# Moving the softmax's power of e behind the layer-norm statistics, and reordering the first tiles' copies, in a correlation and feed-forward kernel

## The chip, the cores and the metric

The kernel runs on one core of a Trainium2 chip. A core has five engines with an instruction queue each: TensorE (PE: matmuls and transposes, with PEld for its weight loads), VectorE (DVE), ScalarE (ACT), GpSimd (POOL) and SyncE (SP, which here only issues DMA transfers). Each engine runs its own queue strictly in order and waits for others by semaphores. The metric is the device time of one execution in microseconds (us).

## The reference

The input x is 2 x 2048 rows of 1024 floats, treated as 4096 rows. Each row is layer-normalised; then two things are made of it and multiplied.

```python
xn = layernorm(x)                              # over the 1024 columns
# s: autocorrelation of a row by FFT, its 6 largest lags, softmax over them,
#    and the sum of the row rolled by those lags with these weights
corr = irfft(rfft(xn) * conj(rfft(xn)))
weights, delay = top_k(corr, 6)
p = softmax(weights)
s = sum_k p[k] * roll(xn, -delay[k])
# g: a gated feed-forward net with rank-2 additions (LoRA); every weight is a
#    quarter-size matrix tiled four times: w = tile(wq, (1, 4))
lin = lambda x, wq, A, B: x @ w.T + 0.5 * (x @ A.T @ B.T)
g = silu(lin(silu(lin(xn, w1q, a1, b1)) * lin(xn, w3q, a3, b3), w2q, a2, b2))
out = x + s * g
```

All is float32.

## The kernel before, in words

**Tiles and macros.** The 4096 rows are worked in 8 macros of 512 rows, each of four tiles of 128 rows. For each macro there is a `Corr` object, which normalises, transposes, finds the lags and the softmax weights, and an `Ffn` object, which runs the feed-forward net. The two are pipelined: while the net of macro m runs, the `Corr` of macro m + 1 is prepared.

**Steps.** A macro is 15 steps (`STEPS`). Steps 0 to 9 each do two of the 20 large products of the first layer (`Ffn.up`, matmuls at L521), step 10 the rest of that layer (`up_rest`), steps 11 to 14 the second layer for one tile of rows each (`Ffn.down`, L589 and L600, then `out`). The schedule is manual: each engine executes its instructions in the order in which the Python code emits them. `plan` fills four lists for each step: `pre` is emitted before a step's matmuls, `mid` and then `half` between its two products, and `end` behind them. Between them stand the gathers: `begin` issues indirect DMAs from GpSimd's queue that fetch rolled rows (at most four in flight), and `sum` adds a fetched row to `s` (ScalarE for the first of six, L471, VectorE for the others, L474). `sums` says how many are added in a step, as a pair: between the products (with `half`), and at the end.

**A tile of the next macro.** `stats` computes mean and variance (VectorE, L171 to L175), then the reciprocal deviation with a power on GpSimd (L177) and the shift (L179, GpSimd). `norm` then normalises on ScalarE (L186), scales the row sum on GpSimd (`rest`, L187), folds halves of the row on VectorE (L191; L142 and L143 in `fold_a`, which give `yc`; L142 uses `rest`) and on GpSimd (L193; L131 and L132 in `fold_b`). `save` writes the row twice to DRAM for the gathers. `turn` transposes the folded tile on TensorE (L215), and ScalarE copies it out of PSUM. `power` multiplies with Fourier tables (L365, L366) and squares (L375 to L381), `lags` goes back to the correlation (L393 to L412), `search` takes the top values and their places (L419 to L423).

**Softmax.** `weights` subtracts the row's largest value (VectorE, L431) and raises e to the result on GpSimd (L433, 24 values per row). `weights_rest` adds up and divides on VectorE (L439 to L443). Before the change, `weights` of macro m + 1 is emitted at the very end of macro m's step 14, and `weights_rest` at the end of step 0 of macro m + 1. In macro 0 they stand in `half` of step 6 and `mid` of step 7.

**The first macro.** It has no earlier macro to hide under. `norm_first`, `back_first` and `turn_first` do its four tiles in the main body (L717 to L744), `fold_lora` sums LoRA inputs on GpSimd, `lora_sum_first` and `lora_first` compute the LoRA part. The weights of the first layer have to be lessened by their first column block once (`lessen`: L136 on VectorE, L137 on GpSimd, two of six parts before the steps begin). `yU` is a second copy of `yT` whose first row differs. Within macro 0 the lags of its own four tiles and the statistics of macro 1's four tiles share steps 0 to 8; `stats` and `norms` in `plan` give the places of the latter.

**At the end of the first layer** `up_rest` makes the last part (L559 to L566), `lora_mid` adds the LoRA part to it (L573, VectorE) and copies it (L576, ScalarE), and L600 multiplies it.

**PSUM.** Two banks (`bank`) serve transposes, powers and lags in turn; five others (`full`) serve the products of the net, which ScalarE seeds (L499) two products ahead.

Of the kernel before, what the change touches and what calls it, by code (L numbers as in the profile page):

```python
# [34 lines left out]
F32 = mybir.dt.float32  # L35
# [12 lines left out]
RT = 4  # L48
# [19 lines left out]
def block_kernel(ctx: ExitStack, tc: tile.TileContext, x, w13t, w0t, w5t, w2t, a13, b13, b5, a2t, tf, ti, pick, out):  # L68
# [23 lines left out]
    def full(name):  # L92

        return psf.tile([P, 512], F32, tag="psf", name=name)
# [61 lines left out]
    class Corr:  # L156
# [96 lines left out]
            nc.scalar.copy(self.yT[0:1, 0, :], acc[0:1, :])  # L253
            nc.scalar.copy(self.yU[0:1, :], acc[32:33, :])

        def again(self):

            self.yU = p1.tile([P, NR], F32, tag="yU", name=f"yU_{self.m}")
            nc.scalar.copy(self.yU, self.yT[:, 0, :])

# [18 lines left out]
        def turn_first(self, r, signs):  # L281
            m = self.m
            if r == 0:
                self.yT = p2.tile([P, 2, NR], F32, tag="yT", name=f"yT_{m}")
                self.cT = p1.tile([P, 2, NR], F32, tag="cT", name=f"cT_{m}")
                self.bT = p1.tile([P, 4, NR], F32, tag="bT", name=f"bT_{m}")
                self.some = p1.tile([P, NR], F32, tag="us", name=f"us_{m}")
            cols = slice(r * P, (r + 1) * P)
            b, yc, back = self.parts.pop(r)

            t = full(f"t1_{m}_{r}")
            for k, (at, sign) in enumerate(((0, 1), (1, 1), (2, 0), (1, 0))):
                for h, (src, e) in enumerate(((b, ident), (back, signs[sign]))):
                    times = bass.AP(src.tensor, src.offset + at, [list(src.ap[0]), [2, P]])
                    nc.tensor.matmul(t[:, k * P : (k + 1) * P], lhsT=times, rhs=e, start=(h == 0), stop=(h == 1))
            nc.scalar.copy(self.bT[:, :, cols], t.rearrange("p (k n) -> p k n", k=4))
            t = full(f"t0_{m}_{r}")
            for k in range(4):
                nc.tensor.transpose(t[:, k * P : (k + 1) * P], yc[:, k, :], ident)
            t3 = t.rearrange("p (k n) -> p k n", k=4)  # L300
            nc.scalar.copy(self.yT[:, :, cols], t3[:, 0:2, :])
            nc.scalar.copy(self.cT[:, :, cols], t3[:, 2:4, :])

        def lora_sum_first(self, r, count):
            cols = slice(r * P, (r + count) * P)
# [12 lines left out]
        def lora_first(self, ffn):  # L318

            m = self.m  # L320
            self.yU = p1.tile([P, NR], F32, tag="yU", name=f"yU_{m}")
            nc.gpsimd.tensor_copy(self.yU, self.yT[:, 0, :])
            self.second = p1.tile([P, 2, NR], F32, tag="second", name=f"second_{m}")
            self.u = p1.tile([P, NR], F32, tag="u", name=f"u_{m}")
            self.pwy = p1.tile([P, 2, NR], F32, tag="pwy", name=f"pwy_{m}")
            ec = p1.tile([P, NR], F32, tag="ec", name=f"ec_{m}_0")
            e2 = p1.tile([P, NR], F32, tag="e2", name=f"e2_{m}_0")
            o2 = p1.tile([P, NR], F32, tag="o2", name=f"o2_{m}_0")

            def on_all(i):  # L330

                acc = full(f"second_{m}_{i}")
                col = pick_sb[:, 2 * i + 1 : 2 * i + 2]
                every = bass.AP(col.tensor, col.offset, [list(col.ap[0]), [0, P]])
                nc.tensor.matmul(acc, lhsT=every, rhs=self.some, start=True, stop=True)
                return acc

            e = full(f"fe_{m}_0")
            nc.tensor.matmul(e, lhsT=tf_sb[:, 0, :], rhs=self.yT[:, 0, :], start=True, stop=True)
            nc.scalar.copy(ec, e)  # L340
            nc.scalar.activation(e2, e, AF.Square)
            gate = on_all(0)
            nc.vector.tensor_copy(self.second[:, 0, :], gate)
            acc = full(f"u_{m}")
            nc.tensor.matmul(acc, lhsT=pick_sb, rhs=self.some, start=True, stop=True)
            nc.vector.tensor_copy(self.yT[0:1, 0, :], acc[0:1, :])
            nc.vector.tensor_copy(self.yU[0:1, :], acc[32:33, :])
            nc.vector.tensor_copy(self.u, acc)
            o = full(f"fo_{m}_0")
            nc.tensor.matmul(o, lhsT=tf_sb[:, 1, :], rhs=self.yT[:, 1, :], start=True, stop=True)  # L350
            nc.vector.tensor_tensor(self.pwy[:, 1, :], ec, o, ALU.mult)
            up = on_all(1)
            ffn.seed(0, (0,))
            nc.scalar.copy(self.second[:, 1, :], up)
            ffn.seed(0, (1,))
            nc.scalar.activation(o2, o, AF.Square)
            nc.gpsimd.tensor_tensor(self.pwy[:, 0, :], e2, o2, ALU.add)
            ffn.seed(1)
# [258 lines left out]
    def plan(m, st, nxt, after, gathers, ffn_next):  # L617

        pre, mid, half, end = ([[] for _ in range(STEPS)] for _ in range(4))
        first = m == 0  # L620
        sums = [(1, 0)] * 7 + [(1, 2)] * 3 + [(1, 1), (0, 0), (2, 1), (2, 1), (0, 0)]
        sums[10] = (0, 0)
        sums[0], sums[1] = (0, 0), (1, 1)
        sums[8], sums[9], sums[11], sums[14] = (2, 1), (2, 1), (1, 0), (1, 0)
        if first:
            sums = [(0, 0)] * 7 + [(1, 1), (2, 2)] + [(2, 1)] * 5 + [(3, 0)]
            mid[0].append(lambda: st.power(1))
            pre[1].append(lambda: st.power(2))
            mid[1].append(lambda: st.power(3))
            for r in range(RT):  # L630
                look(st, r, mid[2 + r], end[2 + r], gathers)
            half[2 + RT].append(st.weights)
            mid[3 + RT].append(st.weights_rest)
            for c in range(2, FULL + 1):
                pre[(0, 0, 1, 3)[c - 2]].append(lambda c=c: load_first(c))
                end[2 * c - 3].append(lambda c=c: lessen_part(c))
        else:
            end[0].append(st.weights_rest)
        if nxt is not None:
            if first:  # L640
                loads, norms, turns = (None, None, None, 3), (0, 1, 5, 6), (pre[6], mid[6], pre[7], pre[8])
                stats = (half[0], half[1], end[4], half[6])

                tags = (("yc", "bcs"), ("zf4", "zf5"), ("e2", "o2"), ("yc", "bcs"))
            else:
                loads, norms, turns = (None, None, 1, 3), (0, 2, 4, 6), (pre[2], pre[4], pre[6], pre[8])
                stats = (half[0], end[1], end[3], end[5])
                tags = (("yc", "bcs"),) * RT
            for r in range(RT):
                if loads[r] is not None:  # L650
                    pre[loads[r]].append(lambda r=r: nxt.load(r))
                stats[r].append(lambda r=r: nxt.stats(r))
                end[norms[r]].append(lambda r=r: (nxt.norm(r, tags[r]), nxt.save(r)))
                turns[r].append(lambda r=r: nxt.turn(r))
            mid[8].append(nxt.lora_sum)
            pre[9].append(lambda: nxt.power(0))
            mid[9].append(lambda: nxt.power(1))
            pre[10].extend([lambda: nxt.power(2), nxt.again])
            mid[10].append(lambda: nxt.power(3))
            pre[11].append(nxt.lora_spread)  # L660
            for r in range(RT):
                look(nxt, r, mid[MID + 1 + r], end[MID + 1 + r], gathers)
            end[STEPS - 1].append(nxt.weights)
            mid[STEPS - 1].insert(0, lambda: (ffn_next.seed(0), ffn_next.seed(1, (0,))))
            end[STEPS - 1].insert(0, lambda: ffn_next.seed(1, (1,)))
        if after is not None:
            pre[MID + 2].append(lambda: after.load(0))
            pre[MID + 4].append(lambda: after.load(1))
        return pre, mid, half, end, sums
# [24 lines left out]
    with tc.manual_schedule():  # L694
# [22 lines left out]
        constants()  # L717
        nc.gpsimd.memset(wide[:, 512:513], 0.0)
        nc.gpsimd.tensor_scalar(negative, ident, -1.0, None, ALU.mult)
        fold_lora(nat)  # L720
        bs = (b[:, :], wide[:, :])
        ycs = [p1.tile([P, 4, P], F32, tag=tag, name=f"yc_{tag}") for tag in ("yc", "zf0")]
        backs = [p1.tile([P, 257], F32, tag=tag, name=f"back_{tag}") for tag in ("bcs", "zf2")]
# [1 line left out]
        st.stats(0)  # L725
        st.stats(1)
        norm(0)
        st.back_first(0, backs[0][:, :])
        st.stats(2)
        norm(1)  # L730
        for r in range(RT):
            st.turn_first(r, (ident, negative))
            if r + 1 < RT:
                st.back_first(r + 1, backs[(r + 1) % 2][:, :])
            if r + 3 < RT:
                st.stats(r + 3)
            if r + 2 < RT:
                norm(r + 2)
            if r == 2:
                st.lora_sum_first(0, 3)  # L740
        st.lora_sum_first(3, 1)
        nc.vector.tensor_copy(basef, base)
        lessen_part(0)
        lessen_part(1)  # L744
        then.load(0)
# [156 lines left out]
```

## Time and profile before

| what | value |
|---|---|
| time, median of 3 runs | 1178.87 us (1176.96 to 1180.08) |
| the profiled execution: time, and span in its trace | 1178.45 us, 1176.7 us |
| granted TensorE clock, mean | 0.998 |
| TensorE busy | 1150.0 us (98%) |
| GpSimd busy | 783.2 us (67%) |
| VectorE busy | 738.7 us (63%) |
| ScalarE busy | 556.5 us (47%) |
| L433, the power of e, 8 times | 4202 ns each |
| L177, the power of the statistics, 32 times | 539 to 1559 ns, median 578 |
| first L521 matmul | starts at 34.22 us |
| a macro in steady state | 142.6 us from one L433 to the next (338.58 to 481.18) |

The times in the rows of the trace are counted in us from the start of the span. In a timeline row the first number is the start, the second the length, then engine, line, operation, output and input, shape; in brackets the idle time of that engine just before, and what ended it. In a row of waits the numbers are the total in us, how often, and the longest. The busy share is an average over 1177 us: which wait costs time has to be read at its place.

### The profile page before, as it was taken

What the parts mean: (1) busy time and instruction counts of PE and PEld (TensorE: products, weight loads), DVE (VectorE), ACT (ScalarE), POOL (GpSimd) and SP (SyncE); (2) the same over time, 40 slices, a digit from 0 to 9 for tenths busy, and PEclk for the clock granted to TensorE, in tenths of its full rate; (3) what the DMA queues carried; (4) which work ended last, traced back from release to release, by engine and by line L of the source; (5) the groups of instructions that cost most, each with busy time, mean ns of one, the idle gap of its engine ahead of it and who ended that gap; (6) DMA issues with size and microseconds to landing.
All of it is one profiled execution on the core that took longest, in us unless ns stands there. A gap on an engine that the chain in (4) does not pass through costs nothing.

```text
span 1176.7 us, 11238 instructions
## 1 busy us (share of the span) xinstructions
PE 1150.0 (98%) x3604; PEld 510.4 (43%) x3604; DVE 738.7 (63%) x985; ACT 556.5 (47%) x981; POOL 783.2 (67%) x643
## 2 busy tenths in 40 slices
PE   5999999999999999999999999999999999999997
PEld 4454344444444444444444444444444443444433
DVE  6587677664676557665576564675548664663455
ACT  4656425664256632565326652366433663344511
POOL 4668867777477755777558784597746877464653
PEclk9999999999999999999999999999999999999999
DMA  9942477533555435454365443654445534452334
GB/s 365 371 135 90 143 242 257 194 131 124 198 178 179 161 126 188 172 177 162 108 224 185 145 165 118 236 179 143 154 146 201 179 127 160 134 188 90 116 117 160
DMA packets 64915, 201.98 MB, mean 172 GB/s; under 512 B 7484, under 2 KB 7868, under 8 KB 64088
## 3 DMA queue, kind: packets, MB, share of 16 engines
q0 software_dynamic: 27648, 100.68, 26.0%
q1 hardware_dynamic: 37208, 100.59, 23.9%
q8 instruction: 28, 0.46, 0.2%
q14 instruction: 31, 0.25, 0.1%
HBM read 150.85 MB, written 50.39 MB: 171 GB/s over the span
## 4 chain that ended last, share of the span: by engine, by line
PE 85%; POOL 5%; DVE 4%; DMA 2%; ACT 2%; issue 1%; SPq 0%; POOLq 0%; DVEq 0%
PE gu L521 37%; PE y L589 24%; PE gu L547 5%; PE u L504 4%; PE y L600 3%; POOL e L433 3%; PE e L393 2%; PE fo L366 2%; PE fe L365 2%; PE t L215 2%; PE o L393 1%; DMA w<-in_w0t 1%; PE ua L231 1%; ACT x L186 1%; DVE where L421 1%
## 5 line engine op out<-in xcount | busy, mean ns | idle before, releaser
L521 PE MATMUL gu<-yT,w_sb 128*128 128x512 f32 x960 | 455.9, 596 | 0.0
L589 PE MATMUL y<-w_sb,zf 128*128 128x512 f32 x640 | 287.4, 596 | 0.0
L521 PEld LDWEIGHTS gu<-yT,w_sb 128*128 128x128 f32 x960 | 176.9, 190 | 227.2 <-issue 208.2
L457 POOL DMA_INDIRECT roll<-scr,lag x192 | 224.4, 1169 | 71.5 <-DVE s L474 28.8
L474 DVE SCALAR_TENSOR_TENSOR s<-roll,w,s 128x1024 f32<-128x1024 f32 x160 | 240.4, 1502 | 9.0 <-DMA roll<-scr,lag 4.1
L499 ACT ACTIVATE gu<-second,b_sb 128x512 f32<-128x512 f32 x320 | 207.6, 685 | 10.0 <-DVE z L528 9.4
L528 DVE TENSOR_TENSOR z<-z,gu 128x512 f32<-128x512 f32 x160 | 108.8, 683 | 159.3 <-PE gu L521 103.6
L613 POOL TENSOR_TENSOR g<-g,x 128x512 f32<-128x512 f32 x62 | 104.6, 1704 | 131.1 <-DVE g L612 108.7
L589 PEld LDWEIGHTS y<-w_sb,zf 128*128 128x128 f32 x640 | 117.3, 190 | 147.0 <-issue 146.3
L526 ACT ACTIVATE z<-gu 128x512 f32<-128x512 f32 x160 | 95.2, 595 | 167.5 <-PE gu L521 167.5
L521 PE MATMUL gu<-yU,w_sb 128*128 128x512 f32 x320 | 163.4, 592 | 0.0
L533 POOL TENSOR_TENSOR zf<-zf,z 128x512 f32<-128x512 f32 x80 | 133.6, 1670 | 19.6 <-DVE z L528 18.7
L531 POOL TENSOR_TENSOR zf<-z,z 128x512 f32<-128x512 f32 x40 | 50.7, 1266 | 76.6 <-DVE z L528 76.6
L521 PEld LDWEIGHTS gu<-yU,w_sb 128*128 128x128 f32 x320 | 60.8, 190 | 76.6 <-issue 72.5
L612 DVE TENSOR_TENSOR g<-s,g 128x512 f32<-128x512 f32 x64 | 41.5, 688 | 78.2 <-ACT g L611 78.2
L611 ACT ACTIVATE g<-y 128x512 f32<-128x512 f32 x64 | 34.7, 594 | 91.5 <-PE y L600 75.0
L547 PE MATMUL gu<-yT,w_sb 128*128 128x512 f32 x128 | 57.6, 593 | 0.0
L191 DVE TENSOR_TENSOR a<-x 128x512 f32<-128x512 f32 x28 | 32.8, 1172 | 29.6 <-ACT x L186 29.6
L504 PE MATMUL u<-z,a_sb 128*2 128x512 f32 (+1 forms) x384 | 49.9, 591 | 0.0
L412 ACT COPY corr<-corr 128x511 f32<-128x511 f32 x32 | 19.8, 618 | 63.2 <-DVE corr L411 63.2
L186 ACT ACTIVATE x<-x,shift,rstd 128x1024 f32<-128x1024 f32 x28 | 34.5, 1233 | 25.6 <-POOL shift L179 25.6
L375 ACT COPY ec<-fe 128x512 f32<-128x512 f32 x31 | 18.0, 581 | 60.0 <-PE fe L365 56.1
(168 smaller groups left out, 1262.8 us busy)
## 6 DMA issues: line engine op xcount, KB each, us to landing
scr<-x SPq DMA_DIRECT2D x64, 512.0 KB
x<-in_x SPq DMA_DIRECT2D x32, 512.0 KB
x<-in_x SPq DMA_DIRECT2D x64, 256.0 KB
out<-g SPq DMA_DIRECT2D x64, 256.0 KB
w_sb<-in_w13t SPq DMA_DIRECT2D x5, 1024.0 KB
second<-rows SPq DMA_DIRECT2D x14, 256.0 KB
w_sb<-in_w2t SPq DMA_DIRECT2D x1, 3072.0 KB
roll<-scr,lag POOLq DMA_INDIRECT x192, 5.9
```

Source lines behind the costliest of these rows:

```text
L457: nc.gpsimd.indirect_dma_start(out=g, out_offset=None, in_=st.scratch[r].rearrange("p (n o) -> (p n) o", o=1), in_offset=bass.IndirectOffs ...
L474: nc.vector.scalar_tensor_tensor(s, g, w, s, ALU.mult, ALU.add)
L499: nc.scalar.activation(acc, self.st.second[:, wi, :], AF.Copy, scale=b13_sb[:, c, q : q + 1])
L504: nc.tensor.matmul(self.u2[32 * j : 32 * j + 2, :], lhsT=a2_sb[:rows, 4 * c + j, :], rhs=z[:rows, :], start=(c == 0), stop=(c == FULL),)
L521: nc.tensor.matmul(acc, lhsT=w13_sb[:, c, 2 * j + wi, k, :], rhs=y, start=False, stop=(k == 1), skip_group_check=True,)
L526: nc.scalar.activation(z, accs[0], AF.Silu)
L528: nc.vector.tensor_tensor(z, z, accs[1], ALU.mult)
L531: nc.gpsimd.tensor_tensor(self.sum_of(c), zs[0], zs[1], ALU.add)
L533: nc.gpsimd.tensor_tensor(self.zf[c], self.zf[c], z, ALU.add)
L547: nc.tensor.matmul(acc, lhsT=w5_sb[:, k, j, :], rhs=self.st.yT[:, k, :], start=(k == 0), stop=False)
L589: nc.tensor.matmul(acc, lhsT=self.zf[c][:, rc], rhs=w2_sb[:, c, d * 512 : (d + 1) * 512], start=(c == 0), stop=False)
L613: (nc.vector if last else nc.gpsimd).tensor_tensor(g, g, xs[d], ALU.add)
```

## The change

The change edits the order in which instructions are emitted, and no arithmetic.

- In macros 1 to 7, `weights` moves from the end of the macro before to `half` of step 0, behind the statistics of the next macro's first tile, and `weights_rest` from the end of step 0 to `mid` of step 1. In macro 0, `weights` moves from `half` of step 6 to the end of step 5.
- In macro 0, `stats(2)` moves from the end of step 4 to the end of step 2, `norm(2)` from the end of step 5 to the end of step 4, `stats(3)` from `half` of step 6 to `half` of step 5; the sums of steps 8 to 11 change from (2, 2), (2, 1), (2, 1), (2, 1) to (2, 1), (1, 1), (2, 2), (2, 2).
- In the start, `turn_first` emits its TensorE work at once and returns its ScalarE copies as two functions, which the main body places: tile 2 is normalised between them, tile 3 ahead of tile 1's copies. `fold_lora` comes behind the first two tiles. The copy of `yU` goes into GpSimd's queue ahead of the lessening of the weights.

```diff
--- before.py
+++ after.py
@@ -253,10 +253,10 @@
             nc.scalar.copy(self.yT[0:1, 0, :], acc[0:1, :])
             nc.scalar.copy(self.yU[0:1, :], acc[32:33, :])
 
-        def again(self):
+        def again(self, copy=nc.scalar.copy):
 
             self.yU = p1.tile([P, NR], F32, tag="yU", name=f"yU_{self.m}")
-            nc.scalar.copy(self.yU, self.yT[:, 0, :])
+            copy(self.yU, self.yT[:, 0, :])
 
 
 
@@ -288,18 +288,24 @@
             cols = slice(r * P, (r + 1) * P)
             b, yc, back = self.parts.pop(r)
 
-            t = full(f"t1_{m}_{r}")
+            tb = full(f"t1_{m}_{r}")
             for k, (at, sign) in enumerate(((0, 1), (1, 1), (2, 0), (1, 0))):
                 for h, (src, e) in enumerate(((b, ident), (back, signs[sign]))):
                     times = bass.AP(src.tensor, src.offset + at, [list(src.ap[0]), [2, P]])
-                    nc.tensor.matmul(t[:, k * P : (k + 1) * P], lhsT=times, rhs=e, start=(h == 0), stop=(h == 1))
-            nc.scalar.copy(self.bT[:, :, cols], t.rearrange("p (k n) -> p k n", k=4))
+                    nc.tensor.matmul(tb[:, k * P : (k + 1) * P], lhsT=times, rhs=e, start=(h == 0), stop=(h == 1))
             t = full(f"t0_{m}_{r}")
             for k in range(4):
                 nc.tensor.transpose(t[:, k * P : (k + 1) * P], yc[:, k, :], ident)
-            t3 = t.rearrange("p (k n) -> p k n", k=4)
-            nc.scalar.copy(self.yT[:, :, cols], t3[:, 0:2, :])
-            nc.scalar.copy(self.cT[:, :, cols], t3[:, 2:4, :])
+
+            def copy_b():
+                nc.scalar.copy(self.bT[:, :, cols], tb.rearrange("p (k n) -> p k n", k=4))
+
+            def copy_y():
+                t3 = t.rearrange("p (k n) -> p k n", k=4)
+                nc.scalar.copy(self.yT[:, :, cols], t3[:, 0:2, :])
+                nc.scalar.copy(self.cT[:, :, cols], t3[:, 2:4, :])
+
+            return copy_b, copy_y
 
         def lora_sum_first(self, r, count):
             cols = slice(r * P, (r + count) * P)
@@ -318,8 +324,6 @@
         def lora_first(self, ffn):
 
             m = self.m
-            self.yU = p1.tile([P, NR], F32, tag="yU", name=f"yU_{m}")
-            nc.gpsimd.tensor_copy(self.yU, self.yT[:, 0, :])
             self.second = p1.tile([P, 2, NR], F32, tag="second", name=f"second_{m}")
             self.u = p1.tile([P, NR], F32, tag="u", name=f"u_{m}")
             self.pwy = p1.tile([P, 2, NR], F32, tag="pwy", name=f"pwy_{m}")
@@ -623,23 +627,21 @@
         sums[0], sums[1] = (0, 0), (1, 1)
         sums[8], sums[9], sums[11], sums[14] = (2, 1), (2, 1), (1, 0), (1, 0)
         if first:
-            sums = [(0, 0)] * 7 + [(1, 1), (2, 2)] + [(2, 1)] * 5 + [(3, 0)]
+            sums = [(0, 0)] * 7 + [(1, 1), (2, 1), (1, 1), (2, 2), (2, 2), (2, 1), (2, 1), (3, 0)]
             mid[0].append(lambda: st.power(1))
             pre[1].append(lambda: st.power(2))
             mid[1].append(lambda: st.power(3))
             for r in range(RT):
                 look(st, r, mid[2 + r], end[2 + r], gathers)
-            half[2 + RT].append(st.weights)
+            end[1 + RT].append(st.weights)
             mid[3 + RT].append(st.weights_rest)
             for c in range(2, FULL + 1):
                 pre[(0, 0, 1, 3)[c - 2]].append(lambda c=c: load_first(c))
                 end[2 * c - 3].append(lambda c=c: lessen_part(c))
-        else:
-            end[0].append(st.weights_rest)
         if nxt is not None:
             if first:
-                loads, norms, turns = (None, None, None, 3), (0, 1, 5, 6), (pre[6], mid[6], pre[7], pre[8])
-                stats = (half[0], half[1], end[4], half[6])
+                loads, norms, turns = (None, None, None, 3), (0, 1, 4, 6), (pre[6], mid[6], pre[7], pre[8])
+                stats = (half[0], half[1], end[2], half[5])
 
                 tags = (("yc", "bcs"), ("zf4", "zf5"), ("e2", "o2"), ("yc", "bcs"))
             else:
@@ -652,6 +654,10 @@
                 stats[r].append(lambda r=r: nxt.stats(r))
                 end[norms[r]].append(lambda r=r: (nxt.norm(r, tags[r]), nxt.save(r)))
                 turns[r].append(lambda r=r: nxt.turn(r))
+        if not first:
+            half[0].append(st.weights)
+            mid[1].append(st.weights_rest)
+        if nxt is not None:
             mid[8].append(nxt.lora_sum)
             pre[9].append(lambda: nxt.power(0))
             mid[9].append(lambda: nxt.power(1))
@@ -660,7 +666,6 @@
             pre[11].append(nxt.lora_spread)
             for r in range(RT):
                 look(nxt, r, mid[MID + 1 + r], end[MID + 1 + r], gathers)
-            end[STEPS - 1].append(nxt.weights)
             mid[STEPS - 1].insert(0, lambda: (ffn_next.seed(0), ffn_next.seed(1, (0,))))
             end[STEPS - 1].insert(0, lambda: ffn_next.seed(1, (1,)))
         if after is not None:
@@ -717,7 +722,6 @@
         constants()
         nc.gpsimd.memset(wide[:, 512:513], 0.0)
         nc.gpsimd.tensor_scalar(negative, ident, -1.0, None, ALU.mult)
-        fold_lora(nat)
         bs = (b[:, :], wide[:, :])
         ycs = [p1.tile([P, 4, P], F32, tag=tag, name=f"yc_{tag}") for tag in ("yc", "zf0")]
         backs = [p1.tile([P, 257], F32, tag=tag, name=f"back_{tag}") for tag in ("bcs", "zf2")]
@@ -725,21 +729,33 @@
         st.stats(0)
         st.stats(1)
         norm(0)
-        st.back_first(0, backs[0][:, :])
+        back = lambda r: st.back_first(r, backs[r % 2][:, :])
+        turn = lambda r: st.turn_first(r, (ident, negative))
+        back(0)
         st.stats(2)
         norm(1)
-        for r in range(RT):
-            st.turn_first(r, (ident, negative))
-            if r + 1 < RT:
-                st.back_first(r + 1, backs[(r + 1) % 2][:, :])
-            if r + 3 < RT:
-                st.stats(r + 3)
-            if r + 2 < RT:
-                norm(r + 2)
-            if r == 2:
-                st.lora_sum_first(0, 3)
+        back(1)
+        fold_lora(nat)
+        st.stats(3)
+        copy_b, copy_y = turn(0)
+        copy_b()
+        norm(2)
+        copy_y()
+        copies = turn(1)
+        back(2)
+        norm(3)
+        for copy in copies:
+            copy()
+        copies = turn(2)
+        back(3)
+        for copy in copies:
+            copy()
+        st.lora_sum_first(0, 3)
+        for copy in turn(3):
+            copy()
         st.lora_sum_first(3, 1)
         nc.vector.tensor_copy(basef, base)
+        st.again(nc.gpsimd.tensor_copy)
         lessen_part(0)
         lessen_part(1)
         then.load(0)
```

## The prediction

> **What bounds the kernel now.** I read the page's busy shares first, then TensorE's waits, then the timelines around each wait, engine by engine.
>
> ```profile
> PE 1150.0 (98%) x3604; PEld 510.4 (43%) x3604; DVE 738.7 (63%) x985; ACT 556.5 (47%) x981; POOL 783.2 (67%) x643
> PE t L295 <- POOL rest L268: 9.8, 1, 9.8
> PE t L215 <- DVE yc L143: 3.5, 7, 0.5
> PE t L215 <- DVE yc L142: 1.7, 1, 1.7
> PE fo L366 <- DVE pwy L378: 1.0, 1, 1.0
> ```
>
> TensorE is the bound: its work is unchanged, so only its waits can move the time. After the first matmul they are few: in the ready macros (m = 1 to 6) one of 0.5 us each, at `turn(0)`, and nothing else; in the first macro 2.2 at `turn(3)` (1.7 + 0.5), 1.0 in `power(1)`, 0.4 earlier; and holes in the start. So all that can be gained after the start is 6 x 0.5 + 3.6 = 6.6 us, while a step that becomes late in a ready macro costs six times.
>
> GpSimd (POOL), VectorE (DVE) and TensorE at the edge of macros 3 and 4 (start, length, engine, line):
>
> ```profile
> 481.18 4.20 POOL L433 TENSOR_TENSOR e<-euler,e 128x24 f32<-128x24 f32 x1 [0.35 <-DVE e L431]
> 485.37 0.54 POOL L177 TENSOR_TENSOR rstd<-var,mhalf 128x1 f32<-128x1 f32 x1
> 486.02 0.26 POOL L179 TENSOR_SCALAR shift<-mv,rstd 128x1 f32<-128x1 f32 x1
> 486.25 1.27 POOL L531 TENSOR_TENSOR zf<-z,z 128x512 f32<-128x512 f32 x1
> 487.74 0.73 POOL L187 TENSOR_SCALAR rest<-rest 128x1 f32<-128x1 f32 x1 [0.22 <-ACT x L186]
> ...
> 483.17 0.16 DVE L175 TENSOR_SCALAR var<-mv 128x1 f32<-128x1 f32 x1
> 487.68 0.69 DVE L191 TENSOR_TENSOR a<-x 128x512 f32<-128x512 f32 x1 [1.66 <-ACT x L186]
> 488.50 1.51 DVE L142 SCALAR_TENSOR_TENSOR yc<-a,rest 128x256 f32<-128x256 f32 x1
> 489.93 1.07 DVE L143 TENSOR_TENSOR yc<-a 128x256 f32<-128x256 f32 x1
> ...
> 491.06 0.44 PE L215 MATMUL t<-ident,yc 128*128 128x128 f32 x2 [0.49 <-DVE yc L143]
> ```
>
> The reader is to see a chain with no slack: `rest` (POOL) frees `yc` (DVE, 488.50), whose end frees the transposes. `rest` waited for ScalarE only 0.22 us; before it POOL was busy. All eight powers of e last 4.20 us.
>
> The start, and the tightest place of the first macro:
>
> ```profile
> 22.46 5.29 POOL L137 TENSOR_TENSOR w_sb<-w_sb,w 128x1024 f32<-128x1024 f32 x2
> 23.16 2.37 DVE L142 SCALAR_TENSOR_TENSOR yc_zf<-a,rest 128x256 f32<-128x256 f32 x1
> 25.45 2.58 DVE L143 TENSOR_TENSOR yc_zf<-a 128x256 f32<-128x256 f32 x1
> ...
> 151.57 1.27 DVE L474 SCALAR_TENSOR_TENSOR s<-roll,w,s 128x1024 f32<-128x1024 f32 x1
> 152.87 2.84 DVE L573 SCALAR_TENSOR_TENSOR zf<-u,zf 2x512 f32<-2x512 f32 x4
> 155.75 0.62 ACT L576 COPY zf<-zf 64x512 f32<-64x512 f32 x1 [7.93 <-DVE zf L573]
> ...
> 156.33 1.21 PE L600 MATMUL y<-w_sb,zf 64*128 64x512 f32 x4
> ```
>
> The lessening of the first weights (L137) meets the last tile's fold: L142 and L143 need 0.49 and 0.42 us elsewhere and take 4.95 here. And at 156.33 TensorE starts as its operand ends (156.37).
>
> **The change, part by part.** *(1) Power of e behind the statistics, macros 1 to 6.* Removed: 4.20 us ahead of `rstd`. Added: 4.20 us behind `shift`, with L531, `rest`, L193, L131, L132 queued behind it. Var is ready at 483.33; `rstd` (0.57, with hand-over 0.1) and `shift` (0.27) end at 484.2, so ScalarE normalises from 484.2 instead of 486.32 and its `x` is there at 485.6. But POOL is in the power from 484.2 to 488.4, and `rest` needs POOL. Does `a` (L191, two operands from SBUF) run meanwhile? L191 took 2.71 us at 58.82, when POOL's L137 (58.62, 2.36) had begun first, and ended 0.55 after it: it stood still for all of it. [...] No row shows the long power beside such an instruction. [...] power to 488.4, `a` to 489.0, L531 to 490.2, `rest` (0.24 where nothing hinders it, 93.57) to 490.5; L142 starts 2.0 us later than 488.50. Without it: L531 to 489.65, `rest` to 489.9; 1.4 later. I take 2.0. TensorE arrives at 490.16 in both cases and the wait has nothing beside it: 6 x 2.0 = **+12.0** (8.4 by the low end).
>
> [...]
>
> Weights_rest (three DVE instructions of 0.18) moves to mid[1], behind L142, L143 and z; ScalarE's first `s` waits for it until about 494.2 (it began at 489.26), with Silu and the seeds of the fifth product behind it, ready near 497.3; TensorE, itself 2.0 late, wants them at 498.5. Nothing added; if that cover fails, 0.5 to 1 us a macro.
>
> *(2) The start.* `fold_lora` (POOL 5.78 to 6.70) leaves the front: `rstd` starts at 5.9 instead of 6.66, everything 0.8 earlier. At its new place its four small POOL instructions meet L142/L143 of tile 1, and ScalarE's `a_sb` behind them (about 15.5) stands ahead of `copy_b(0)` and tile 2's `x`: tile 2 is normalised 0.7 later than before (15.34). Tile 3 gains: its `x` no longer waits behind copies (18.4 instead of 20.36), and the yU copy, now ahead of the lessening in POOL's queue, waits for the last yT, so the lessening can't meet the fold: L143 ends near 21.8 instead of 28.03. What is late next is ScalarE: back(3) and the copies of tiles 1 and 2 to about 22.2, the LoRA product (1.65) to 23.7, `turn(3)` (2.4) to 26.1, yT near 26.2 instead of 28.56. **-2.4**. The bounds: TensorE's holes from 9.8 to 34 add up to about 3.1, with the 0.8 at most -3.9; +0.5 if `a_sb` holds more. VectorE's lessening (2.8 us) moves to 22 to 25, free time. POOL's (2 x 2.4) runs from 27, the first done by 29.5, while the first product wants it near 32. SP issues the same transfers in the same order (each norm's two saves move along with it, past no other transfer); DMA is full until 55 us, but the next w0 tile, landing near 50 (19.4 MB moved by then), is wanted near 52.
>
> *(3) Norm(2) at end[4], stats(2) at end[2], stats(3) at half[5].* Norm(2) puts a 1.3 us pass on ScalarE and L191, L142, L143 (about 3.2 us [...]) on DVE ahead of z and corr of lag tile 3, while only stats(2) (1.7) leaves that spot. Corr ended at 87.37 and TensorE's `turn(0)`, which takes its bank of PSUM, came at 88.92: slack 1.55. I get corr 2.7 later: **+1.1** (0 to 2). Power(e) then starts some 3 us earlier against TensorE, and stats(3) is out of its way: `rest` of norm(3) ends near 104.9 instead of 106.57, TensorE arrives 1.1 later: of 2.2 at `turn(3)`, **-1.9**.
>
> *(4) Sums rearranged.* One `s` fewer at the end of step 8: `pwy` is no longer held by the 2.92 us `s` at 123.59: **-1.0**. One more `s` at the end of step 10 stands between L566 and L573 (the last of the rows above), where TensorE has 0.0 of slack: **+1.3**, by the 1.27 of the row; 0 if DVE has come free earlier[...].
>
> Sum: 12.0 - 2.4 + 1.1 - 1.9 - 1.0 + 1.3 = **+9.1**. The profiled execution took 1178.45 (span 1176.7), 0.4 under the median 1178.87: 1178.45 + 9.1 = 1187.5.
>
> **Rivals.** *Harmless power (not slower).* If the power is over before `rest` is wanted, the six waits vanish: 6 x -0.5 - 2.9 (the other five terms) = -5.9, 1172.5. It decides at a power of 4.2 - 2.0 = 2.2 us for no loss; for it speaks that `x` does come 2.1 earlier; against it that eight durations agree to 2 ns. Chance 0.09. *All of the first macro.* The start brings 3.9, (3) and (4) cost nothing and save 3.2[...]: 8.4 - 7.1 = +1.3, 1179.8, no change. Each is at its bound, so 0.08. *Knock-on.* The late `s` delays seeds or the next statistics: another 0.8 a macro, 9.1 + 4.8 = +13.9, 1192.4. For it speaks a slack of 1.2 us; chance 0.11. *As summed*, own range 1183 to 1190.5: 0.72.
>
> **How the numbers follow.** 1187.5 is the likeliest case. From 1181.5 (low end of the power's cost, larger gains at the start) to 1191.5 leaves out the first rival, most of the second and half of the third. A measurement here can tell about 0.3% (3.5 us): faster 0.09, within 0.08, slower 0.83.
>
> **What would show it.** Right: TensorE's waits at L215 for DVE yc grow to about 2.5 us each, six times; L433 starts behind L179; L142 of the last first-macro tile near 0.5 us; first L521 near 31.8 instead of 34.22; a wait of about 1.3 at L600 once. Wrong: L433 under 2.2 us, `rest` directly behind `shift`, or waits at L215 unchanged.

## The result, and the profile after

The changed kernel takes 1188.36 us (median of 6 runs, 1186.66 to 1188.77) against 1177.55 for the kernel before in the same comparison: ratio 1.0084, 95% interval 1.0071 to 1.0097. The time is inside the range, 0.9 us from the forecast. But two terms of the sum were off by about 5 and 3.5 us in opposite directions. The forecast also started from one execution of the kernel before, 1178.45, which was 0.9 us above the median; the difference itself is 10.8 us where 9.1 was forecast. So the closeness of the total is partly luck.

In kernels that contain the new start, lines from there on have moved, those from `weights` on by 4: the power of e is L437, the first layer's products are L525, L600 has become L604, L573 and L576 are L577 and L580, and the gathers and sums are L461, L475 and L478.

The page's busy shares and TensorE's waits of the kernel after:

```profile
PE 1153.0 (97%) x3604; PEld 511.0 (43%) x3604; DVE 733.1 (62%) x985; ACT 554.8 (47%) x981; POOL 785.0 (66%) x643
PE t L215 <- DVE yc L142: 8.4, 6, 1.8
PE t L215 <- DVE yc L143: 2.9, 6, 0.5
PE t L215 <- DVE corr L415: 1.3, 1, 1.3
PE y L604 <- DVE zf L577: 0.7, 1, 0.7
```

The reader is to see three things. A wait for L142 has come in each of the six ready macros. The waits at `turn(3)` and in `power(1)` are gone and two new ones of the first macro stand in their place. And TensorE is busy 3.0 us longer with the same 3604 instructions, which no list of waits explains.

The same place as in the prediction's timelines, which by the numbering from 0 is the edge of macros 2 and 3, in the timelines of GpSimd, VectorE and TensorE (start, length, engine, line):

```profile
484.96 0.26 POOL L179 TENSOR_SCALAR shift<-mv,rstd 128x1 f32<-128x1 f32 x1
485.19 4.18 POOL L437 TENSOR_TENSOR e<-euler,e 128x24 f32<-128x24 f32 x1
489.35 1.25 POOL L535 TENSOR_TENSOR zf<-z,z 128x512 f32<-128x512 f32 x1
490.59 0.23 POOL L187 TENSOR_SCALAR rest<-rest 128x1 f32<-128x1 f32 x1
...
486.63 0.69 DVE L191 TENSOR_TENSOR a<-x 128x512 f32<-128x512 f32 x1 [1.51 <-ACT x L186]
490.85 1.52 DVE L142 SCALAR_TENSOR_TENSOR yc<-a,rest 128x256 f32<-128x256 f32 x1 [3.53 <-POOL rest L187]
...
490.16 1.02 PE L525 MATMUL gu<-yT,w_sb 128*128 128x512 f32 x2
492.52 0.41 PE L215 MATMUL t<-ident,yc 128*128 128x128 f32 x2 [1.33 <-DVE yc L142]
493.41 0.44 PE L215 MATMUL t<-ident,yc 128*128 128x128 f32 x2 [0.49 <-DVE yc L143]
494.40 3.34 PE L525 MATMUL gu<-yT,w_sb 128*128 128x512 f32 x4
```

The power now stands between `shift` and `rest`. `x` is ready early, VectorE has `a` by 487.3, and then waits 3.53 us for `rest`. The last row is the surprise: the same four matmuls took 1.88 us before and take 3.34 now. The row of the kernel before:

```profile
492.04 1.88 PE L521 MATMUL gu<-yT,w_sb 128*128 128x512 f32 x4
```

The windows of 2 us over that place, in the kernel after (us, busy of PE, PEld, DVE, ACT, POOL, granted TensorE clock, DMA share, GB/s):

```profile
492.00:494.00 2.00, 0.99 (x6) 0.62 (x6) 2.00 (x4) 0.00 (x0) 1.92 (x3) 1.00 0.01 4
494.00:496.00 2.00, 1.95 (x6) 0.98 (x6) 1.27 (x3) 0.62 (x1) 1.83 (x3) 0.67 0.00 0
496.00:498.00 2.00, 2.00 (x4) 0.84 (x3) 0.96 (x2) 2.00 (x4) 0.66 (x2) 0.50 0.29 49
498.00:500.00 2.00, 2.00 (x8) 0.49 (x10) 2.00 (x3) 2.00 (x6) 2.00 (x1) 0.98 0.55 213
```

After the long wait TensorE's granted clock falls to half (0.67 and 0.50 in the second and third row) for 3.41 us. In this execution it happens in macros 1, 3 and 6; before the change no 2 us window ahead of the last matmuls shows it. From the first product to the matmul behind the two products' half (L508) it took 5.22 us (494.40 to 499.62) against 3.53 (492.04 to 495.57) before: 1.7 us for each drop.

The start: the last tile's fold no longer meets the lessening.

```profile
20.99 0.48 DVE L142 SCALAR_TENSOR_TENSOR yc_zf<-a,rest 128x256 f32<-128x256 f32 x1
21.39 0.42 DVE L143 TENSOR_TENSOR yc_zf<-a 128x256 f32<-128x256 f32 x1
...
31.70 1.88 PE L525 MATMUL gu<-yT,w_sb 128*128 128x512 f32 x4
```

And the end of macro 0's first layer, with two sums ahead of L577:

```profile
145.79 0.68 DVE L570 TENSOR_TENSOR zf<-zf,z 64x512 f32<-64x512 f32 x1 [2.21 <-POOL zf L569]
146.40 2.59 DVE L478 SCALAR_TENSOR_TENSOR s<-roll,w,s 128x1024 f32<-128x1024 f32 x2
149.03 2.84 DVE L577 SCALAR_TENSOR_TENSOR zf<-u,zf 2x512 f32<-2x512 f32 x4
...
151.93 1.77 PE L604 MATMUL y<-w_sb,zf 64*128 64x512 f32 x4 [0.71 <-DVE zf L577]
```

A cleaner measure than the listed waits is the distance, from start to start, of equal places. From the first matmul of step 11 (L589 or L593) to that of the next macro, in us:

| kernel | macro 0 to 1 | 1 to 2 | 2 to 3 | 3 to 4 | 4 to 5 | 5 to 6 |
|---|---|---|---|---|---|---|
| before | 142.68 | 142.60 | 142.59 | 142.61 | 142.58 | 142.61 |
| after | 147.50 | 143.94 | 145.67 | 143.97 | 143.95 | 145.68 |

Those with a clock drop are the first, third and last: 143.95 is a macro with the longer wait, 145.67 one with the wait and a drop.

### The profile page after: what moved, and what is told of

Read it like the earlier page. It is cut to its first block, busy times and chain, and to the rows that moved or that the text cites. A ratio compares the mean times of both kernels' runs of the same rounds, so it can differ in the third digit from the quotient of the medians.

```text
span 1186.5 us, 11239 instructions
## 1 busy us (share of the span) xinstructions
PE 1153.0 (97%) x3604; PEld 511.0 (43%) x3604; DVE 733.1 (62%) x985; ACT 554.8 (47%) x981; POOL 785.0 (66%) x643
## 4 chain that ended last, share of the span: by engine, by line
PE 85%; POOL 6%; DVE 5%; ACT 2%; issue 1%; DMA 0%; DVEq 0%; POOLq 0%
PE gu L525 39%; PE y L593 23%; PE gu L551 4%; PE u L508 4%; PE y L604 3%; PE e L397 2%; PE fe L369 2%; POOL e L437 2%; PE fo L370 2%; PE t L215 2%; PE o L397 1%; DVE stats L171 1%; PE ua L231 1%; DVE where L425 1%; DVE top L423 1%
## 5 line engine op out<-in xcount | busy, mean ns | idle before, releaser
L525 PE MATMUL gu<-yT,w_sb 128*128 128x512 f32 x960 | 460.4, 601 | 0.0
L593 PE MATMUL y<-w_sb,zf 128*128 128x512 f32 x640 | 287.4, 596 | 0.0
L525 PEld LDWEIGHTS gu<-yT,w_sb 128*128 128x128 f32 x960 | 178.1, 191 | 228.9 <-issue 208.5
L461 POOL DMA_INDIRECT roll<-scr,lag x192 | 218.6, 1138 | 71.5 <-DVE s L478 28.8
L478 DVE SCALAR_TENSOR_TENSOR s<-roll,w,s 128x1024 f32<-128x1024 f32 x160 | 236.4, 1477 | 5.4 <-DMA roll<-scr,lag 2.5
L593 PEld LDWEIGHTS y<-w_sb,zf 128*128 128x128 f32 x640 | 117.3, 190 | 147.1 <-issue 146.3
L525 PE MATMUL gu<-yU,w_sb 128*128 128x512 f32 x320 | 163.9, 594 | 0.0
L537 POOL TENSOR_TENSOR zf<-zf,z 128x512 f32<-128x512 f32 x80 | 138.8, 1736 | 26.8 <-DVE z L532 25.3
L525 PEld LDWEIGHTS gu<-yU,w_sb 128*128 128x128 f32 x320 | 61.5, 192 | 78.0 <-issue 73.1
L475 ACT ACTIVATE s<-roll,w 128x1024 f32<-128x1024 f32 x32 | 36.5, 1142 | 51.1 <-DVE w L447 49.7
L142 DVE SCALAR_TENSOR_TENSOR yc<-a,rest 128x256 f32<-128x256 f32 x28 | 40.9, 1461 | 30.7 <-POOL rest L187 28.7
L508 PE MATMUL u<-z,a_sb 128*2 128x512 f32 (+1 forms) x384 | 49.9, 591 | 0.0
L191 DVE TENSOR_TENSOR a<-x 128x512 f32<-128x512 f32 x28 | 31.1, 1110 | 24.6 <-ACT x L186 24.6
```

Source lines behind the costliest of these rows:

```text
L461: nc.gpsimd.indirect_dma_start(out=g, out_offset=None, in_=st.scratch[r].rearrange("p (n o) -> (p n) o", o=1), in_offset=bass.IndirectOffs ...
L478: nc.vector.scalar_tensor_tensor(s, g, w, s, ALU.mult, ALU.add)
L508: nc.tensor.matmul(self.u2[32 * j : 32 * j + 2, :], lhsT=a2_sb[:rows, 4 * c + j, :], rhs=z[:rows, :], start=(c == 0), stop=(c == FULL),)
L525: nc.tensor.matmul(acc, lhsT=w13_sb[:, c, 2 * j + wi, k, :], rhs=y, start=False, stop=(k == 1), skip_group_check=True,)
L537: nc.gpsimd.tensor_tensor(self.zf[c], self.zf[c], z, ALU.add)
L593: nc.tensor.matmul(acc, lhsT=self.zf[c][:, rc], rhs=w2_sb[:, c, d * 512 : (d + 1) * 512], start=(c == 0), stop=False)
```

## Experiments

Theory: the power of e in its new place costs, by holding GpSimd ahead of `rest` and by what TensorE's clock does after the longer wait; the start and the first macro gain. Rivals: the cost sits in the first macro; it is the order on other engines and not GpSimd's time; the clock drops are unrelated to the wait.

**The move of the power alone.**

```diff
-        else:
-            end[0].append(st.weights_rest)
...
+        if not first:
+            half[0].append(st.weights)
+            mid[1].append(st.weights_rest)
...
-            end[STEPS - 1].append(nxt.weights)
```

> The kernel before, with the move of the power of e in macros 1 to 7 alone (weights behind the statistics of step 0, weights_rest in the middle of step 1); start and first macro as before. Theory (the power costs, twice): TensorE's wait at L215 goes from 0.5 to 1.8 us in six macros, +8.0 to 8.4 us, and in two to four of the six the granted clock drops to about half for some 3.4 us after it, +1.7 us each: together +11.5 to +15, so 1189 to 1193. Rival (the added time sits in the changed start and first macro): within 3 us of the kernel before, about 1178.

Measured: 1187.5 us (1187.27 to 1190.25), ratio 1.0091, interval 1.0076 to 1.0107. The waits of the ready macros are those of the kernel after, 1.3 and 0.5 us, with those of the old first macro beside them. The macros are 143.94 to 144.06 apart, one, with a clock drop, 145.66. The profiled run has that one drop, fewer than the two to four expected, and the median is 1.5 us under the expected band. Its row of waits, with macro 0's old wait as the seventh:

```profile
PE t L215 <- DVE yc L142: 9.5, 7, 1.7
```

The cost of the change is in this edit; the rival is out.

**The start and first macro alone** (the kernel after with the power back).

```diff
+        if not first:
+            end[0].append(st.weights_rest)
...
-        if not first:
-            half[0].append(st.weights)
-            mid[1].append(st.weights_rest)
...
+            end[STEPS - 1].append(nxt.weights)
```

> The kernel after, with the power of e back at the end of the macro before and weights_rest at the end of step 0; the new start and first macro stay. Theory (start and first macro gain): start -2.5, turn(0) +1.3, turn(3) -2.2, power(1) -1.0, L604 +0.7, no clock drop: -3.7 against before, about 1174, with the six waits of 0.5 us at L215 still there. Rival (the start only looks shorter and is given back later): 1177.5, no difference from before.

Measured: 1175.19 us, ratio 0.9979 (0.9972 to 0.9987). A gain, but 2.1 us and not 3.7; its macros 1 to 6 are 142.60 apart as before, without a drop. The missing part is in the start, below.

**The start alone** (the kernel before with the new first tiles, `fold_lora` and the yU copy; the plan as before).

> The kernel before with the new start alone (first tiles, fold_lora, the yU copy); plan and power of e as before. Theory: L143 of the last first tile takes 0.4 us and the first L525 starts 0.8 to 2.5 us earlier, the rest unchanged with its waits of 1.7 and 0.5 us at turn(3) and 1.0 in power(1): 1174.8 to 1176.5. Rival (the start's gain comes from the clock of TensorE, which warmed up early in one profile and late in the other, not from the edit): 1177.3.

Measured: 1176.37 us, ratio 0.9989 (0.9982 to 0.9996). The start gains 1.0 us. Its first L525 is at 31.70, as in the kernel after, 2.5 before the 34.22 of the first profile; but that profile was itself of a late execution (1178.45, and the median of before is 1177.41 over 28 runs). The rows of TensorE, two of the kernel before, then two of the kernel after, show why: pairs of these matmuls take 0.63 us at first and 0.40 later, which is called warming up below.

```profile
18.23 0.63 PE L295 MATMUL t<-ident,back_zf 128*128 128x128 f32 x2
...
19.32 0.40 PE L295 MATMUL t<-ident,b 128*128 128x128 f32 x2
...
12.19 0.63 PE L295 MATMUL t<-ident,back_bcs 128*128 128x128 f32 x2
...
13.44 0.40 PE L295 MATMUL t<-ident,b_other 128*128 128x128 f32 x2
```

The first pair of 0.40 us comes 9.5 us after the first matmul in one, 4.4 in the other. In the run with the power moved alone, whose start is the old one, it came 4.2 us after a first matmul at 10.89, and its first product started at 33.45. So a part of the 2.5, about 0.8 us (34.22 against 33.45), is when TensorE warmed up. The rival is right about that part and wrong about the rest.

**The old sums in the first macro** (the kernel with start and first macro alone, steps 8 to 11 as before).

```diff
-            sums = [(0, 0)] * 7 + [(1, 1), (2, 1), (1, 1), (2, 2), (2, 2), (2, 1), (2, 1), (3, 0)]
+            sums = [(0, 0)] * 7 + [(1, 1), (2, 2)] + [(2, 1)] * 5 + [(3, 0)]
```

> The kernel of the run with the start and first macro alone, with the sums of steps 8 to 11 of macro 0 as before the change. Theory: the wait at L604 goes (-1.35 us from start to start) and that in power(1), L370, comes back (+1.3): nothing to see in the time, 1175.2, but both waits change places in the trace. Rival (the s of step 10 isn't what holds L577): L604 still waits.

Measured: 1174.76 us, ratio 0.9969 (0.9958 to 0.9980), 0.4 under the run with the new sums. Its waits show the exchange: none at L604, and

```profile
PE fo L370 <- DVE pwy L382: 1.0, 1, 1.0
```

is back. Moving a sum from step 8 to step 10 only moved the wait.

**A shorter power.** The kernel after, with the power over one tile's 6 values instead of four tiles' 24 in macros 1 to 7. It leaves out the power for the other three tiles.

```diff
-        def weights(self):
+        def weights(self, tiles=RT):
...
-            every = bass.AP(euler.tensor, euler.offset, [list(euler.ap[0]), [0, RT], [0, TOP]])
-            nc.gpsimd.tensor_tensor(self.e, every, self.e, ALU.pow)
+            every = bass.AP(euler.tensor, euler.offset, [list(euler.ap[0]), [0, tiles], [0, TOP]])
+            nc.gpsimd.tensor_tensor(self.e[:, :tiles], every, self.e[:, :tiles], ALU.pow)
...
-            half[0].append(st.weights)
+            half[0].append(lambda: st.weights(1))
```

> The kernel after, with the power of e in macros 1 to 7 taken over 6 values a row instead of 24 (the softmax weights of three of four tiles are left unfinished). From 0.57 us for one value and 4.2 for 24, some 1.4 us for six. Theory (what counts is how long GpSimd is held between shift and rest): L187 comes 2.8 us earlier, so ScalarE's x frees it, all waits at L215 in macros 1 to 6 vanish with the clock drops, about 1171. Rival (the order of emission on DVE, ScalarE and TensorE, such as the late weights_rest, does it, not GpSimd's time): waits of 1.8 us remain, 1188.

Measured: 1169.2 us, ratio 0.9928 (0.9913 to 0.9944). The order of emission is the same on all engines; only the length is not:

```profile
479.00 1.35 POOL L437 TENSOR_TENSOR e<-euler,e 128x6 f32<-128x6 f32 x1
```

All waits at L215 in macros 1 to 6 are gone, and the clock drops too: no 2 us window ahead of 1162 us is under 1.00. It is GpSimd's time between `shift` and `rest` that costs. The macros are 141.57 apart, 1.03 less than before the change, though the list put the old wait at 0.49: the listed idle time begins at a matmul's modelled end (here the next pair starts at 484.82, ahead of the 484.99 at which the one before it ends), and it hides about half of the stall.

**The wait filled.** The kernel after with two idle matmuls ahead of `turn(0)`, in the bank that it overwrites.

```diff
+                if i == 0 and r == 0 and m > 1:
+                    nc.tensor.matmul(t, lhsT=ident, rhs=w2_sb[:, 0, :512], start=True, stop=True)
+                    nc.tensor.matmul(t[:, :256], lhsT=ident, rhs=w2_sb[:, 0, :256], start=True, stop=True)
```

> The kernel after, with idle matmuls on TensorE (identity by a piece of w2, one of 512 and one of 256 columns, 1.3 us) ahead of turn(0) in macros 1 to 6, written to the bank that turn(0) then overwrites; they take the place of the first 1.3 us of the wait, and L142 still ends it. Theory (it is TensorE's idleness in the wait that makes the granted clock drop, at 1.7 us a time): the macros keep their 143.9 us each, no window of 2 us between 40 and 1150 us shows a granted clock under 0.97, and the two or three drops of the kernel after are gone: 1183.3 to 1185. Rival (the clock drops for another reason, and the two are only neighbours): the drops stay, 1187 to 1189. If the idle matmuls are not hidden by the wait: up to 6 x 1.3 us more.

Measured: 1183.19 us (1182.85 to 1183.58), ratio 1.0042 (1.0026 to 1.0057): 5.2 us under the kernel after, with more work on TensorE. Its timeline at the edge of macros 2 and 3, where the added lines make the transposes L218 and the products L528:

```profile
489.41 1.02 PE L215 MATMUL t<-w_sb,ident 128*128 128x512 f32 x2
490.27 0.59 PE L216 MATMUL t<-w_sb,ident 128*128 128x256 f32 x2
490.82 0.44 PE L218 MATMUL t<-ident,yc 128*128 128x128 f32 x2
491.81 0.44 PE L218 MATMUL t<-ident,yc 128*128 128x128 f32 x2 [0.55 <-DVE yc L143]
492.08 0.87 PE L218 MATMUL t<-ident,bcs 128*128 128x128 f32 x4
492.79 1.88 PE L528 MATMUL gu<-yT,w_sb 128*128 128x512 f32 x4
```

The macros stay 143.97 to 144.20 apart, the next product takes 1.88 us again, and no 2 us window ahead of 1176 us shows a lower clock. With the idle time in the wait filled, the drops of the kernel after, three in its trace, are gone: here they go with the idle time.

**The power behind the normalising.** The kernel after with one word changed.

```diff
-            half[0].append(st.weights)
+            end[0].append(st.weights)
```

> The kernel after, with the power of e of macros 1 to 7 emitted behind the normalising of the next macro's first tile (end of step 0) instead of ahead of it; nothing else. Theory (it is the rest, L187, queued behind the power that costs): the waits at L215 in macros 1 to 6 vanish altogether, no clock drop, and against the version with the power at its old place another 6 x 0.5 = 3 us are gained: about 1171. The first row s of a macro then waits for the power, to about where it stands in the kernel after. Rival (the power does harm wherever it stands in step 0 or 1, since DVE's total and ScalarE's first s wait for it and seeds come late): new waits at L525 of 1 us or more a macro, 1177 or more.

Measured: 1196.84 us, ratio 1.0164 (1.0151 to 1.0178): the slowest of all, and the theory's forecast failed by 26 us. The waits at L215 did vanish, but the rival came true in another place. GpSimd, VectorE, ScalarE, VectorE and TensorE in order:

```profile
493.04 4.20 POOL L437 TENSOR_TENSOR e<-euler,e 128x24 f32<-128x24 f32 x1
...
497.27 0.18 DVE L443 TENSOR_REDUCE total<-e 128x4 f32<-128x24 f32 x1 [3.71 <-POOL e L437]
...
498.57 1.15 ACT L475 ACTIVATE s<-roll,w 128x1024 f32<-128x1024 f32 x1 [8.02 <-DVE w L447]
...
500.23 0.69 DVE L532 TENSOR_TENSOR z<-z,gu 128x512 f32<-128x512 f32 x1 [1.70 <-ACT z L530]
...
500.98 1.02 PE L508 MATMUL u<-z,a_sb 128*2 128x512 f32 x2 [2.25 <-DVE z L532]
```

The reader is to follow the chain downwards: the power ends, the weights follow at once, ScalarE's first `s` has waited 8.02 us for them with the Silu of the next product behind it in its queue, the `z` of that Silu comes late, and TensorE stands at L508, with clock drops in four macros. The macros are 145.24 us apart without a drop and about 146.4 with one. The power has a deadline on both sides: it must not stand ahead of `rest`, and the weights must not be late for an `s` that others queue behind.

**All of it together.** The power behind the normalising, weights_rest at the end of step 1, the first `s` in step 2; the sums of steps 9 and 10 and macro 0's `turn` calls moved.

```diff
-        sums[0], sums[1] = (0, 0), (1, 1)
+        sums[0], sums[1], sums[2] = (0, 0), (0, 0), (2, 1)
...
-            sums = [(0, 0)] * 7 + [(1, 1), (2, 1), (1, 1), (2, 2), (2, 2), (2, 1), (2, 1), (3, 0)]
+            sums = [(0, 0)] * 7 + [(1, 1), (2, 1), (2, 1), (2, 1), (2, 2), (2, 1), (2, 1), (3, 0)]
...
-                ..., turns = ..., (pre[6], mid[6], pre[7], pre[8])
+                ..., turns = ..., (mid[6], pre[7], mid[7], pre[8])
...
-            half[0].append(st.weights)
-            mid[1].append(st.weights_rest)
+            end[0].append(st.weights)
+            end[1].append(st.weights_rest)
```

> The kernel after with three edits: the power of e of macros 1 to 7 behind the normalising of the next tile (end of step 0), weights_rest at the end of step 1 and the first s of a macro in step 2 (two there, none in step 1), so that nothing on ScalarE waits for the weights; in macro 0 one more s in step 9 and one fewer in step 10; turn(0) and the two behind it half a step later. Theory: no wait at L215 and none at u L508, macros of 141.6 us as in the run with the power of one tile, no clock drops; L604 and turn(0) of macro 0 give back 1.3 and 1.5 us: 1166 to 1168, faster than every kernel so far. Rival (the weights come too late wherever the power stands behind the normalising): waits of 1 us or more a macro at u L508 or at L525, 1173 or more.

Measured: 1166.48 us (1165.96 to 1167.06), ratio 0.9902 (0.9884 to 0.9920), the fastest of all kernels here and 1.8% under the changed kernel. Behind the first L525 TensorE has a single listed wait, 0.4 us in macro 0; the macros are 141.47 apart. VectorE still waits for the power, but 1.40 us in an idle place, and nothing queues behind it:

```profile
477.74 0.73 POOL L187 TENSOR_SCALAR rest<-rest 128x1 f32<-128x1 f32 x1 [0.23 <-ACT x L186]
481.82 4.20 POOL L437 TENSOR_TENSOR e<-euler,e 128x24 f32<-128x24 f32 x1
...
486.05 0.18 DVE L443 TENSOR_REDUCE total<-e 128x4 f32<-128x24 f32 x1 [1.40 <-POOL e L437]
```

## Why the prediction was right, and where its terms were not

The sum against the two profiled executions, from start to start. An undisturbed stretch over a `turn` or a `power` is 1.73 or 1.72 us; what is over it is the stall.

| step | predicted | measured | from |
|---|---|---|---|
| start | -2.4 | -2.5 in the traces, -1.0 in the runs | 34.22 to 31.70; run with the start alone |
| (1) wait at `turn(0)`, macros 1 to 6 | +12.0 | +8.5 | 5 x 1.34 (143.94 less 142.60), 1.8 in macro 1 |
| clock drops | none | +5.1 | 3 x 1.7 |
| (3) new wait at macro 0's `turn(0)` | +1.1 | +1.5 | L525 to L525 3.24, less 1.73 |
| (3) `turn(3)` | -1.9 | -2.9 | 4.59 to 1.73 |
| (4) `power(1)` | -1.0 | -1.3 | 3.03 to 1.71 |
| (4) L604 | +1.3 | +1.35 | L589 to L589 5.53, L593 to L593 6.88 |
| sum | +9.1 | +9.8 | spans 1176.7 and 1186.5 |

- *The mechanism* was right at every place named: the power behind `shift`, `rest` queued behind it, `yc` and the transposes late; six waits; corr late for `turn(0)`'s bank; `turn(3)` (by more than forecast, as `rest` ended at 102.7 and not at 104.9) and `power(1)` freed; L604 pushed by a sum. The runs with the power alone and with the short power show the first, the one with old sums the last two; the corr place was seen in the trace and answered in the combined kernel, not isolated.
- *The term that was mis-sized* is step (1), by VectorE's `a`. The prediction let the power hold it back for its whole length, as one row had shown it beside another GpSimd instruction (L191 at 58.82 took 2.71 us beside L137); that it would be so beside the power was the author's estimate. The row decides against it here: L191, with both inputs in SBUF, started at 486.63 in the middle of the power and took 0.69 us, as at that place before, and so it did in all six macros (691 to 693 ns). So the low end held: +1.34 a macro where that end said 1.4. Beside the lessening of 128 x 1024 elements VectorE did take longer: L142 and L143 of the last first tile took 4.95 us before, with L137 running, and 0.90 after, clear of it. And in macro 0 of the kernel after, where VectorE's two-input L136 began first, the power took 5.16 us, 1 us longer than the other seven. That the two instructions hold each other up was not isolated:

```profile
93.16 1.28 DVE L136 SCALAR_TENSOR_TENSOR w_sb<-w,minus,w_sb 128x1024 f32<-128x1024 f32 x1
...
93.32 5.16 POOL L437 TENSOR_TENSOR e<-euler,e 128x24 f32<-128x24 f32 x1 [1.25 <-DVE e L435]
```

- *The term that was missing* is the clock: the step "its work is unchanged, so only its waits can move the time" put it at nothing. The traces show where the drops fall. Each lasts 3.41 us, and their starts (204.54, 494.68 and 928.17 in the kernel after; 355.10, 501.87, 648.64 and 938.78 with the power behind the normalising) lie 85, 127, 43, 43 and 85 times 3.413 us apart. So in each of the two traces the drops begin on one grid of 3.413 us, from the first drop to the last. These are the windows of that grid that end where the three drops start and, for the other three macros, the least busy ones over the wait (columns as above; the first number after the length is TensorE's busy time):

```profile
201.13:204.54 3.41, 1.10 (x7) 0.62 (x6) 3.20 (x5) 0.00 (x0) 3.33 (x5) 1.00 0.32 123
347.90:351.31 3.41, 2.23 (x11) 1.31 (x12) 3.34 (x6) 0.00 (x0) 3.33 (x4) 1.00 0.07 25
491.26:494.67 3.41, 1.61 (x9) 1.09 (x10) 3.34 (x6) 0.00 (x0) 3.33 (x4) 1.00 0.15 60
634.62:638.03 3.41, 2.23 (x6) 0.68 (x4) 1.51 (x2) 0.00 (x0) 3.33 (x5) 1.00 0.88 280
781.40:784.81 3.41, 2.13 (x10) 1.28 (x11) 3.34 (x6) 0.00 (x0) 3.33 (x4) 1.00 0.04 17
924.76:928.17 3.41, 1.53 (x10) 1.08 (x10) 3.34 (x6) 0.00 (x0) 3.33 (x4) 1.00 0.26 90
```

The first, third and last, 1.10 to 1.61 us busy, were followed by a drop; the others, with 2.13 us and more, were not. In the other runs the same line divides: the power alone dropped behind 1.57 and not behind 2.08 and 2.14, the power behind the normalising dropped behind 1.16 to 1.41 and not behind 1.61 and 1.74. So in these traces a drop goes with where the wait falls in the grid. In the kernel after, a wait that straddled an edge left both windows at 2.13 us or more, and as a macro is not a whole number of windows long (143.95 us are 42.2), each had its own place. The windows ahead of the three drops of the kernel after were a third to nearly half busy (1.10 to 1.61 of 3.41 us), and the longest single wait at L215 listed there is 1.8 us.
- *The old wait* was undersized too. The prediction took 0.5 us a macro from the list and 6.6 us as all that could be gained behind the start; the macros of the combined kernel are 1.13 us shorter than before (141.47 against 142.60), and it gained 11 us in all.
- *The start's size* rested on one profile. Its gain in the runs is 1.0 us. The profile of before had warmed up late, which accounts for about 0.8 of the difference; the rest stays open.
- *Rivals.* Harmless power: out, it is what the short power shows, at 1.35 us. All of the first macro: out. Knock-on: ScalarE's `s` did move, from 489.26 to 495.38, and its cover of about a microsecond held, as a macro without a drop grew by no more than the later L142 explains; the run with the power behind the normalising shows the price when it doesn't, 2.6 us a macro, or 3.8 with a drop.

The runs of the kernel after fall into two groups, 1186.66 and 1186.81 at a mean clock of 0.996 and four from 1188.32 to 1188.77 at 0.995: some 1.7 us apart, which is about one drop. The two parts alone add up to +8.1 us where both together cost +10.8, and their profiled executions had one drop against three. Both readings are inferred: drops were counted in one execution of each kernel.

## What to carry to other kernels

An instruction on an engine that is 67% busy can still be the tightest one of a period: before moving it, list what is queued behind it until the next point at which the bounding engine waits, and also who waits for its own result and what is queued behind *that*. The power of e cost 1.1 us a macro at its old place, another 1.3 one place later, and 2.6 to 3.8 more than at the old place two places later; moved together with its consumers it cost TensorE no wait. Price a longer wait on TensorE with the clock drop that may follow it (1.7 us each here), and size waits from start to start of equal places and not from the listed idle time.

## What the hardware did that was not expected

- Stalls of 1.3 and 0.5 us on TensorE, 0.9 us apart, were followed in three of six cases by 3.41 us at half its granted clock, 1.7 us each. Filling the first with 1.3 us of idle matmuls made the kernel 5.2 us faster.
- Whether a stall was followed by a drop went with where it fell in a grid of windows of 3.413 us. In the ten traces, from TensorE's first pair of 0.40 us to its last matmuls, every window with TensorE busy for at most 1.57 us was followed by a drop and none with 1.7 us or more; of two with 1.61 us one was.
- TensorE's warm-up at the start, from its first matmul to the first pair of 0.40 us, took from 3.0 us (the run with the old sums) to 9.5 (the kernel before), although the profile's column of the granted clock says 1.00 until then. With the old start, a first such pair at 19.3 us instead of 15.1 went with a first product 0.8 us later (34.22 against 33.45).
- The power on GpSimd took 0.58 us for one value a row (median of L177), 1.35 for 6 and 4.18 to 4.20 for 24: by these three, about 0.16 us a value. With a two-input VectorE instruction that began behind it, it took 4.18 and that one 0.69, as at its place before; with one that began ahead of it, it took 5.16.
